# Convolution sums on ScalarE and GpSimd, column combinations on VectorE alone, projection products between the last attention steps

## The chip, the core and the metric

The kernel runs on one core of a Trainium2 chip. That core has five engines that work side by side, each through its own queue in order: TensorE (PE in the profile, its weight loads PEld), VectorE (DVE), ScalarE (ACT), GpSimd (POOL) and SyncE (SP, which here issues most of the transfers). The metric is the device time of one execution in microseconds. Before the change it is 2511.84 us, the median of three runs (2492.11 to 2514.36).

## What is computed

The input is `x`, eight images of 32 by 32 positions with 256 channels, all in float32. Cut to what matters:

```python
# layer 0: convolution beside attention with relative positions, on the group-normalized input
g = group_norm(x)
conv = conv3x3(g, conv_w) + conv_b                         # 192 channels
k, q, v = split(g @ qkv_w + qkv_b)                         # 8 heads of 8
w = softmax(q @ k.T + rel_w(q) + rel_h(q))                 # 1024 x 1024 per head and image
x = x + concat([conv, (w @ v) @ attn_w + attn_b])
# layer 1: attention of one head, then two experts per image
t = x.reshape(8, 1024, 256)
n = layer_norm(t)
t = t + n + softmax(Q(n) @ K(n).T / sqrt(128)) @ V(n) @ W_o + b_o
n = layer_norm(t)
out = t + layer_norm(n + top2_experts(n)) 
```

## The kernel before

The images go one after the other through two layers, and the experts of all images follow at the end. One image takes some 243 us. In program order it has these stages:

1. `conv_layer_attention(b)`, the convolution layer's attention. It works in four units of four heads and 512 queries. A loop over `s` (44 steps) runs three things at a distance of ten and eleven steps. `Unit.score` (L588, then the maximum by DVE at L596) finds the maxima of a unit. `Unit.weigh` (L628, exponentials by ACT at L636) makes the weights, and `Unit.gather` (L645) makes the products with the values. For the first ten steps there is nothing to weigh, and products of the convolution stand in between (`conv.run`). In the last eleven steps there is nothing to score, and there the steps of `norm_steps` (the group normalization of the next image) are done through `ahead`. After the last step `settle` divides the last unit by its sums: it transposes `os` to `pa` (L670), DVE takes reciprocals `rc` (L673) and writes `at` (L674). Then `at` is transposed (`tpa`, L744), copied to `aT` (L745), and multiplied by the output projection (`pp`, L750). DVE adds that to the image `T[b]` (L751).
2. `attention_layer(b)`, the second layer's attention. It begins with a normalization over channels: statistics (L762, L86 to L90), then eight tiles `n` (L773) that PE transposes to `tpn` (L777) and ACT copies to `nT` (L781). POOL adds each `n` to `T[b]` (L778). Then come projections (L793, L809), scores (L830), exponentials, transposes (L850) and products (L861, L873). At the end POOL makes a sum over tokens (L913, L915).

While image b is in stage 2, work of image b+1 is put between its steps. `combine()` makes the combinations `gdif` of columns for the convolution (`by_fours`: the convolution along x is done by a scheme with six products for four columns). `fill(us)` takes steps of the generator `input_steps` until the given number of microseconds is used up. These are in turn four products `pk` (L394, for keys and queries, which go to `kq` at L403 by ACT and L410 by DVE, and by 16 transfers on SP to the patterns `km`), eight steps of `pvv` (L425, values, which DVE adds to `vall` at L433), eight pieces of `prel` (L464, position terms, copied by DVE at L476 and ACT at L478, after each of which four or five products of the convolution are run) and four steps of `tpw` (L489, transposes, copied to `rwq` by ACT and DVE in turn). The amounts that a step returns (`yield 0.86, False`) are its assumed duration and whether it is a piece after which convolution products follow.

The convolution itself (`conv_steps`) has two halves `r` of three pairs. A pair is two groups of six products (L511) into one PSUM tile `pc`. After each pair the six-products scheme is undone: the two groups become sum and difference, and these are added with weights to the four column groups `four` of `T[b]`. The first half of an image's convolution runs in the normalization of the image before, with `pc` in the pool `po_tile`, which has one buffer. The second half runs in the first ten steps of its own attention, with `pc` in `st_tile`, which has three. Image 0 does both halves there.

The order of PE's instructions is the order of the program text (`manual_schedule` for PE). On DVE, ACT, POOL and SP a planner orders the instructions when the program is built, by estimated durations and by the order of the text. Before the loop over the images DVE's order is by hand as well; there image 0's combinations are made, with all of `by_fours` on DVE. PSUM tiles come from pools: `st_tile` three buffers, `lg_tile` two, `po_tile` one.

## Time and profile before

| | us |
|---|---|
| median of three runs | 2511.84 |
| lowest and highest run | 2492.11, 2514.36 |
| the profiled execution | 2486.52 |
| its span, first to last instruction | 2483.7 |
| DVE busy | 1531.3 (62%) |
| ACT busy | 995.2 (40%) |
| POOL busy | 501.5 (20%) |

The page comes from one execution. Its groups give, for one line of the program and one engine, the count, the busy time and the mean duration. After the bar stands how long the engine was idle before these instructions and what ended most of that. The groups that the change touches:

```profile
L511 PE MATMUL pc<-convw,gdif 128*128 128x192 f32 x1152 | 235.8, 347 | 18.9 <-DVE sd L535 8.6
L350 DVE SCALAR_TENSOR_TENSOR gdif<-x 128x128 f32<-128x128 f32 x64 | 46.5, 796 | 0.0
L527 POOL TENSOR_TENSOR T<-T,sd 128x384 f32<-128x384 f32 x32 | 31.3, 1003 | 63.7 <-DVE sd L525 63.6
L745 DVE COPY aT<-tpa 64x512 f32<-64x512 f32 x16 | 10.8, 678 | 1.9 <-PE tpa L744 1.1
```

The first line says: 1152 products of the convolution, 235.8 us together, and PE idle for 18.9 us before them, of which 8.6 ended when DVE had written `sd`. A timeline gives instructions in order of time with merged repeats; `[0.93 <-ACT os L662]` means that the engine was idle for 0.93 us and what it then had was `os`, written by ACT. PEclk is the granted clock of TensorE, 1.00 for full rate.

### The profile page before, as it was taken

To read this page: it belongs to the slowest core of one execution; us is meant where nothing else is said; L and a number is where in the kernel's file an instruction comes from. 1 tells how busy PE (TensorE), PEld (TensorE's weight loads), DVE (VectorE), ACT (ScalarE), POOL (GpSimd) and SP (SyncE) were. 2 spreads that over 40 slices of the span, in tenths; PEclk is the share of its full clock that TensorE was granted. 3 is DMA by queue.
4 is the path that set the end of the run, shared out by engine and by line. 5 is a ranking of instruction groups with operands and counts; after the bars stand their busy time and mean duration, and the time that the engine had idled before them with its cause. 6 is when DMAs were issued, how large, how long until landed. Compare 5 with 4: busy or idle time off the path is not lost. (4 is left out here: it accounts for less than half of the span.)

```text
span 2483.7 us, 41827 instructions
## 1 busy us (share of the span) xinstructions
PE 2338.0 (94%) x17273; PEld 1313.9 (53%) x17273; DVE 1531.3 (62%) x2681; ACT 995.2 (40%) x1661; POOL 501.5 (20%) x434
## 2 busy tenths in 40 slices
PE   5999999999989999999999999999998869999998
PEld 4535643564356436643663366336632646666665
DVE  7776487648754875587568746774684444444443
ACT  2254336433643364346334632462256323332232
POOL 3103120402040204111320132022200132222221
PEclk7999999999999999999999999999999979999999
DMA  4520242134213412241224032403240032221110
GB/s 123 80 39 25 40 97 38 36 48 81 33 37 51 85 26 48 57 81 13 53 57 81 9 57 68 71 3 57 51 71 3 1 124 77 76 68 68 68 60 26
DMA packets 71469, 135.83 MB, mean 55 GB/s; under 512 B 12000, under 2 KB 24168, under 8 KB 69232
## 3 DMA queue, kind: packets, MB, share of 16 engines
q1 hardware_dynamic: 65488, 115.47, 23.4%
q0 software_dynamic: 3056, 15.73, 1.8%
q8 instruction: 136, 2.23, 0.4%
q10 hardware_dynamic: 2736, 1.97, 0.3%
q14 instruction: 53, 0.43, 0.1%
HBM read 53.43 MB, written 25.17 MB: 32 GB/s over the span
## 5 line engine op out<-in xcount | busy, mean ns | idle before, releaser
L596 DVE TENSOR_REDUCE my<-lg 128x32 f32<-128x1024 f32 x512 | 618.5, 1223 | 153.6 <-PE st L628 126.0
L636 ACT ACTIVATE PT<-st 128x512 f32<-128x512 f32 (+1 forms) x944 | 541.6, 632 | 412.3 <-PE st L628 407.9
L628 PE MATMUL st<-F,km 32*128 32x512 f32 x2048 | 547.5, 644 | 17.0 <-DMA F<-mb 11.7
L588 PE MATMUL lg<-km,F 24*128 24x512 f32 x2048 | 536.5, 642 | 11.4 <-DVE my L596 7.0
L645 PE MATMUL po<-PT,vall 128*32 128x256 f32 (+1 forms) x3200 | 316.7, 455 | 2.4 <-ACT PT L636 2.4
L588 PEld LDWEIGHTS lg<-km,F 24*128 24x128 f32 x2048 | 155.6, 184 | 191.3 <-issue 109.7
L511 PE MATMUL pc<-convw,gdif 128*128 128x192 f32 x1152 | 235.8, 347 | 18.9 <-DVE sd L535 8.6
L511 PEld LDWEIGHTS pc<-convw,gdif 128*128 128x128 f32 x1152 | 190.3, 195 | 90.4 <-issue 62.9
L645 PEld LDWEIGHTS po<-PT,vall 128*32 128x32 f32 x3200 | 67.0, 108 | 315.0 <-issue 280.9
L628 PEld LDWEIGHTS st<-F,km 32*128 32x128 f32 x2048 | 178.7, 184 | 97.6 <-issue 45.2
L1214 PE MATMUL phd<-n2T,w 128*128 128x512 f32 x512 | 223.8, 595 | 0.0
L1231 PE MATMUL py<-w,hT 128*128 128x256 f32 x1024 | 223.6, 379 | 0.0
L1231 PEld LDWEIGHTS py<-w,hT 128*128 128x128 f32 x1024 | 194.6, 190 | 33.3 <-issue 7.7
L311 POOL TENSOR_TENSOR T<-T,l0b 128x2048 f32<-128x2048 f32 x8 | 36.3, 4539 | 712.9 <-PE tpx L304 712.9
L1238 DVE TENSOR_TENSOR r<-py,n 128x256 f32<-128x256 f32 x64 | 27.1, 423 | 213.0 <-PE py L1231 213.0
L1214 PEld LDWEIGHTS phd<-n2T,w 128*128 128x128 f32 x512 | 97.0, 191 | 115.0 <-issue 107.8
L861 PE MATMUL po<-pt,qkv 128*128 128x256 f32 x512 | 116.6, 381 | 11.3 <-DVE pt L853 11.3
L839 DVE TENSOR_REDUCE nm<-lg 128x1 f32<-128x1024 f32 x64 | 78.1, 1221 | 77.8 <-PE lg L830 77.8
L1221 ACT ACTIVATE hT<-phd,b1c 128x512 f32<-128x512 f32 x128 | 86.3, 686 | 96.5 <-PE phd L1214 96.3
L830 PE MATMUL lg<-qkv 128*128 128x512 f32 x256 | 119.1, 593 | 0.0
L861 PEld LDWEIGHTS po<-pt,qkv 128*128 128x128 f32 x512 | 96.6, 190 | 36.2 <-DVE pt L853 13.2
L778 POOL TENSOR_TENSOR T<-T,n 128x256 f32<-128x256 f32 x64 | 47.2, 743 | 270.5 <-DVE n L773 270.5
(256 smaller groups left out, 2615.7 us busy)
## 6 DMA issues: line engine op xcount, KB each, us to landing
F<-rh SPq DMA_DIRECT2D x256, 128.0 KB
F<-kq SPq DMA_DIRECT2D x256, 64.0 KB
F<-rwd SPq DMA_DIRECT2D x256, 64.0 KB
w<-in_L_ffn_W_dram SPq DMA_DIRECT2D x32, 512.0 KB
rwd<-rw SPq DMA_DIRECT2D x16, 512.0 KB
Td<-T POOLq DMA_DIRECT2D x8, 1024.0 KB, 8.3
T<-Td SPq DMA_DIRECT2D x8, 1024.0 KB
out_dram<-yo SPq DMA_DIRECT2D x16, 512.0 KB
```

The source lines that it names most:

```text
L511: nc.tensor.matmul(pc[:, v, :], lhsT=gflat[:, 2 * pair + v, kc, at : at + P], rhs=convw[:, 2 * pair + v, dy, kc * CO : (kc + 1) * CO], sta ...
L588: nc.tensor.matmul(lg[:, a, :], lhsT=self.F[r : r + 24, a, 0, i * P : (i + 1) * P], rhs=KM[self.g][r : r + 24, a].rearrange("p e k -> p (e ...
L596: nc.vector.tensor_reduce(my[:, :, hl], lg.rearrange("p a (y x) -> p y a x", y=WW), AX.XY, ALU.max)
L628: nc.tensor.matmul(st[:, i, :] if len(heads) > 1 else st, lhsT=KM[self.g][r : r + 32, a, e, :], rhs=self.F[r : r + 32, a, e, :], start=Tru ...
L636: nc.scalar.activation(self.pts[j][:, hs, :], st, AF.Exp)
L645: nc.tensor.matmul(self.po[32 * hl : 32 * hl + 32, cols], lhsT=vall[:, j, h * (DH + 1) : h * (DH + 1) + 32], rhs=self.pts[j][:, hl, cols], ...
L830: nc.tensor.matmul(lg[:, h, :], lhsT=qk[0][:, i * P : (i + 1) * P], rhs=qk[1][:, h * 512 : (h + 1) * 512], start=True, stop=True,)
L839: nc.vector.tensor_reduce(nm, lg, AX.X, ALU.max, negate=True)
L861: nc.tensor.matmul(po[:, 0:IB], lhsT=v1[:, jc, :], rhs=pt[:, jc, :], start=jc == 0, stop=jc == NT - 1)
L1214: nc.tensor.matmul(phd, lhsT=ws[k][0][:, kc, f * P : (f + 1) * P], rhs=n2T[:, kc, q * 512 : (q + 1) * 512], start=kc == 0, stop=kc == KC - 1,)
L1221: nc.scalar.activation(hT[:, k * NF + f, :], phd, AF.Gelu, bias=b1c[:, f, k * B + b : k * B + b + 1])
L1231: nc.tensor.matmul(py, lhsT=hT[:, k * NF + f, j * P : (j + 1) * P], rhs=ws[k][1][:, f, :], start=k == 0 and f == 0, stop=k == TOPK - 1 and ...
```

## The change

Three parts. First, `by_fours` has no other engine to choose: its sums and differences of two tensors, which were on POOL for images 1 to 7, are on DVE for all.

Second, the sums after a pair of convolution products. Before, ACT copied one group and DVE made sum and difference out of PSUM and part of the additions to `four`, POOL the others. Now ACT copies both groups to `m`, and POOL makes all sums from there, with scalings of the second pair by ACT.

Third, `input_steps` of the next image is made before the attention of this one, and a function `more(n)` takes n of its steps. Two `pk` steps stand ahead of the last `settle` and two behind it, and four steps of `pvv` stand ahead of `pp`. One of the two copies `aT` goes to ACT. The first `fill` in the second layer has 4.5 in place of 7.5.

```diff
-        def by_fours(xn, other):
+        def by_fours(xn):
-            two = other.tensor_tensor
+            two = nc.vector.tensor_tensor
...
                             if v and i == n - 1:
-                                if pair < 2:
-                                    neg = work.tile([P, CO], FP, tag="neg", name="neg")
-                                    sd = work.tile([P, 2, CO], FP, tag="sd", name="sd", bufs=2)
-                                if pair == 0:
-                                    nc.scalar.copy(neg, pc[:, 1, :])
-                                    nc.vector.tensor_tensor(sd[:, 0], pc[:, 0, :], neg, ALU.add)
-                                    nc.vector.tensor_tensor(sd[:, 1], pc[:, 0, :], neg, ALU.subtract)
-                                    for h in range(2):
-                                        nc.gpsimd.tensor_tensor(
-                                            four[:, 2 * h : 2 * h + 2], four[:, 2 * h : 2 * h + 2], sd, ALU.add
-                                        )
-                                elif pair == 1:
-                                    nc.scalar.mul(neg, pc[:, 1, :], 2.0)
-                                    nc.vector.scalar_tensor_tensor(
-                                        sd[:, 0], neg, 0.5, pc[:, 0, :], ALU.mult, ALU.add
-                                    )
-                                    nc.vector.scalar_tensor_tensor(
-                                        sd[:, 1], pc[:, 0, :], 2.0, neg, ALU.mult, ALU.subtract
-                                    )
-                                    nc.gpsimd.tensor_tensor(four[:, 0:2], four[:, 0:2], sd, ALU.add)
-                                    nc.vector.scalar_tensor_tensor(
-                                        four[:, 2:4], sd, 4.0, four[:, 2:4], ALU.mult, ALU.add
-                                    )
+                                m = work.tile([P, 2, CO], FP, tag="m", name="m", bufs=2)
+                                nc.scalar.copy(m, pc)
+                                add = nc.gpsimd.tensor_tensor
+                                if pair == 2:
+                                    add(four[:, 0:4:3], four[:, 0:4:3], m, ALU.add)
                                 else:
-                                    nc.vector.tensor_tensor(four[:, 0:4:3], pc, four[:, 0:4:3], ALU.add)
+                                    sd = work.tile([P, 2, CO], FP, tag="sd", name="sd")
+                                    add(sd[:, 0], m[:, 0], m[:, 1], ALU.add)
+                                    add(sd[:, 1], m[:, 0], m[:, 1], ALU.subtract)
+                                    if pair:
+                                        nc.scalar.mul(sd[:, 1], sd[:, 1], 2.0)
+                                    add(four[:, 0:2], four[:, 0:2], sd, ALU.add)
+                                    if pair:
+                                        nc.scalar.mul(m, sd, 4.0)
+                                        sd = m
+                                    add(four[:, 2:4], four[:, 2:4], sd, ALU.add)
...
+                if g == NU:
+                    more(KC)
                 if 0 <= g and g <= NU and l == 0 and g > 0:
                     units[g - 1].settle(at)
+                if g == NU:
+                    more(KC)
...
-                nc.vector.tensor_copy(
-                    aT[:, q * 512 : (q + 1) * 512], tp[0:DK].rearrange("p j t -> p (j t)")
-                )
+                dst, src = aT[:, q * 512 : (q + 1) * 512], tp[0:DK].rearrange("p j t -> p (j t)")
+                if q == 0:
+                    nc.vector.tensor_copy(dst, src)
+                else:
+                    nc.scalar.copy(dst, src)
+            more(NT // 2)
...
-            fill(7.5)
+            fill(4.5)
...
+                steps = iter(()) if last else input_steps(b + 1, held)
+
+                def more(n):
+                    for _ in range(n):
+                        next(steps, None)
+
                 conv_layer_attention(
...
-                steps = iter(()) if last else input_steps(b + 1, held)
```

More of the change, by code (lines that the diff above doesn't have):

```diff
@@ L684, with conv_layer_attention @@
         LAG = 2
-        def conv_layer_attention(b, units, kq, rh, rwd, rwq, conv, early, ahead):
+        def conv_layer_attention(b, units, kq, rh, rwd, rwq, conv, early, ahead, more):
             at = work.tile([P, NT, DK], FP, tag="at", name="at")
@@ L962 @@
             reld_steps()
-            other = chain(by_fours(held["xn"], nc.vector), conv_weights(taps))
+            other = chain(by_fours(held["xn"]), conv_weights(taps))
             for _ in steps:
@@ L992 @@
                     iter(()) if last else ahead(),
+                    more,
                 )
                 conv = Conv(b + 1)
-                steps = iter(()) if last else input_steps(b + 1, held)
                 def fill(us):
@@ L1009, in combine @@
                     if not last:
-                        for _ in by_fours(held["xn"], nc.gpsimd):
+                        for _ in by_fours(held["xn"]):
                             pass
```

## The prediction

> **What bounds the kernel now.** The page comes first: its rows of busy time say TensorE (PE) carries the span, and the row PEclk says where it runs at half rate.

> ```profile
> PE 2338.0 (94%) x17273; PEld 1313.9 (53%) x17273; DVE 1531.3 (62%) x2681; ACT 995.2 (40%) x1661; POOL 501.5 (20%) x434
> PEclk7999999999999999999999999999999979999999
> ```

> So a change pays only where PE stands idle, runs at half clock, or is paced by another engine. From one layer end (L751 starts) to the next an image takes some 243 us, with 10 to 12 us of PE gaps. Three places belong to this change. The first is the end of the convolution layer's attention; here is the timeline of all engines at the end of image 2 (start, us, engine, line, idle before):

> ```profile
> 702.55 0.66 PE L670 MATMUL pa<-ident,os 128*128 128x128 f32 x4 [0.93 <-ACT os L662]
> 702.58 2.16 DVE L350 SCALAR_TENSOR_TENSOR gdif<-x,gdif 128x128 f32<-128x128 f32 x4
> ...
> 703.05 0.60 PE L744 MATMUL tpa<-ident,at 128*64 128x128 f32 x4
> ...
> 704.87 0.24 DVE L673 RECIPROCAL rc<-pa 128x16 f32<-128x16 f32 x1
> ...
> 705.49 1.06 PE L744 MATMUL tpa<-ident,at 128*64 128x128 f32 x4 [1.84 <-DVE at L674]
> ...
> 706.48 3.67 PE L750 MATMUL pp<-aw,aT 64*128 64x64 f32 x16
> ```

> PE waits 0.93 for ACT's `os`, then 1.84 because DVE ends the column combinations (L350) before it takes up `rc`. Afterwards the same four transposes take 1.06, not 0.60, and `pp` 3.67, not 2.00 as in image 1: half clock. The table of busy time by stretch, seven image ends, tells the same (last fields: PEclk, DMA share, GB/s):

> ```profile
> 457.00:475.00 18.00, 16.44 (x159) 11.22 (x155) 13.37 (x44) 7.18 (x11) 5.89 (x7) 1.00 0.04 6
> 700.00:718.00 18.00, 14.93 (x61) 9.47 (x61) 12.29 (x41) 4.91 (x8) 4.41 (x5) 0.72 0.02 3
> ```

> Images 0, 2, 4, 6 end at a clock of 0.81, 0.72, 0.81, 0.72, the odd ones at 1.00; there the wait before L744 is about 0.3 only. The second place is the normalization that follows, where a pair of convolution products waits for its one PSUM buffer (timeline of PE):

> ```profile
> 481.78 0.56 PE L511 MATMUL pc<-convw,gdif 128*128 128x192 f32 x2 [1.16 <-DVE sd L525]
> ...
> 491.71 1.21 PE L511 MATMUL pc<-convw,gdif 128*128 128x192 f32 x6 [1.23 <-DVE sd L535]
> ```

> The third is the first eight score steps, before any exponentials. DVE is busy 23.81 of the 26 us from 556 to 582, and the waits of PE's weight loads from 555 to 591 name it:

> ```profile
> PEld lg L588 <- DVE my L596: 5.8, 9, 1.1
> ```

> DVE paces PE there, so DVE work taken out of this stretch is time.

> [...] in image 0, where DVE alone makes the combinations, four `gdif<-x` take 1.25 us; at 449.31 with Pool beside it eight take 6.27. [...] The trace shows the half rate after gaps of 0.9 and 1.8 us in a row, so low use is enough; cause and phase are not shown. [...] The trace has no GpSimd instruction on PSUM.

> **The change part by part.** Seven image boundaries (0 to 6) have a next image; all sums are over these.

> *Combinations on DVE.* Pool loses 12 sums per image, 13 us. DVE gains them: in image 0 they read 0.63, 0.63, 0.45, 0.46, 0.66, 0.68, 0.51, 0.51, 0.61, 0.56, 0.60, 0.55, together 6.85. The 24 fused ones fall from 12.5 (449.31 to 461.62, with Pool) to 7.0 (image 0's rows). In wall time, image 0's run from 34.77 to 49.48, less the three copies between, is 12.3 us, against 12.5 (449.31 to 461.82). `xn`'s last L333 loses its 1.54 for 0.74. So DVE comes free some 0.9 us earlier, at about 460.9: no cost and no gain by itself, as long as `rc` is needed later than that.

> *Products between the last steps.* Moved up: eight PE instructions of `pk` (3.5 us, 464.95 to 468.49), the two ACT and two DVE writes of `kq` (0.77 and 0.73 each), 16 transfers `km<-kq` on SP (image 0: 11.03 us for 16, with nothing behind them until `rwd<-rw`), and half of `pvv` (1.84 of 3.68). Nothing on POOL's queue moves. `xn` is ready at 449.4, 10 us before. The first `pk` half (1.75) covers the 0.93 for `os`. The second covers `pa` to `at` (0.24 + 0.29 and hand-offs; `pa` now ends near 463.4, after DVE's 460.9). `pvv` covers the copies of `aT`, one of which goes to ACT (0.59). Gain: 7 x 0.93, plus the waits before L744 (1.87, 0.33, 1.84, 0.31, 1.86, 0.26, 1.87, sum 8.3), **15 us**. The moved `kq` writes stand ahead of `aT` on DVE and ACT, 0.7 us each, under the same cover.

> *What their old cover hid.* `fill(7.5)` becomes `fill(4.5)`: behind `pp`, PE has half of `pvv` (1.84) and two pieces of `prel` with their convolution steps (2.6 and 2.9), 7.3 us. DVE needs 0.69 + 2.71 + 0.63 + 0.15, ACT about 0.3, DVE 0.18, then `vall` 0.69 and `n` 0.41: 5.8, or 6.8 if a copy of `prel` (1.06) slips in. Cost 0. But one `prel` piece fewer is left for the eight later slots, so two `tpw` steps now fall between the last transposes, when both `tpn` tiles hold two of three PSUM buffers. The second waits for the first's copy (0.59 ACT), the third partly (0.69 DVE): 0.6 to 1.3 per image, I take 0.9, **-6 us**. Bounds 0 (the free buffer comes earlier) and -12.

> *Convolution sums, normalization half.* One ACT copy frees the PSUM pair. A 128x384 copy is not in the trace; between 128x192 (0.32) and 128x512 (0.59) I read 0.48. The gap of 1.16 and 1.23 (0.32 + 0.36 + 0.35 and hand-offs) becomes about 0.6: 7 x 1.15, **8 us**.

> *Convolution sums, score half.* DVE loses 0.36 + 0.35 (L524, L525) and 0.35 + 0.35 + 0.56 (L532, L535, L539), 1.97 us, inside the DVE-paced stretch; L543 (0.55) lies behind a transfer `F<-mb` and pays nothing. Pool works here longer, and L600 beside it took 0.62, not 0.29: -0.5. 7 x 1.45, **10 us**; bounds 5 and 14. Image 0's half is paced by PE: 0.

> *What is added.* Pool per half: four 192-wide sums (between 0.40 for 128 and 0.73 for 256, I take 0.57) and five 384-wide (1.00), 7.3 against 3.3 now. ACT: three copies, and scalings of 192 and 384, 2.3 against 0.65. ACT has 9.7 busy of 36 us in the normalization, and 2.2 of 36 in the score stretch. New waits: the scaling waits for Pool's two sums, 1.2 us or more if Pool holds an `L778` (0.74) or the running sum of the token mean; behind it on ACT are copies of `prel` and `rwq`. The next use of such a buffer is a piece of 2.6 us or more away: 0. On Pool the sums stand ahead of `T += n` (L778), which frees DVE's two `n`; a hold-up of 3.1 us is under two slots of 3.2. Scoring itself has no exponentials on ACT until 591.3.

> *Clock.* The four half-rate segments at even ends make up (1 - 0.81) x 18 x 2 and (1 - 0.72) x 18 x 2, 34 half-rate us in all, so at most 17 us. Other low spots remain (448, 578), and their phase moves. I take **10**; bounds -10 and 17.

> Sum: 15 - 6 + 8 + 10 + 10 = 37 us. Against the profiled execution's own 2486.5 that is 2449.5. The median of the runs, 2511.84, stands 25 us above it; the same amount gives **2475**.

> **Rivals.** *Given back* (chance 0.28): gaps close but PE waits shortly afterwards, at the `tpw` steps, for ACT behind a Pool wait, or in another half-rate window. For it: low clock turns up at 448 in odd images instead of at their end, at 578 too. Against: PE is nearly solid between. With 15 + 8 + 5 gained, 12 lost at `tpw` and 5 in the clock: 11 us, 2500. That the moved products do not run early, since PE has a written order but DVE and ACT don't, belongs here: it leaves 8 + 10 - 6, also 2500.

> *DVE late behind the combinations* (0.12, slower): DVE's order is planned from estimated costs. With twelve more DVE instructions the planner may leave some of the 12.3 us behind `at`. They then stand ahead of statistics and `n`, whose cover is now 7.3, down from 9.7. It decides once more than 1.5 us of them spill. With 8 us spilled, PE waits 6.5, and a half-rate segment of 10.24 costs 5: 7 x 11.5 = 80, less 37, so 43 slower, 2555. Against: today they are wholly ahead of L673, with 12 us from `xn` to `rc`.

> **How the numbers follow.** The steps hold (0.60): 2445 to 2490 by their bounds, 2475 likeliest. A difference under 1% (2487 to 2537) is about what a measurement of this kernel cannot tell from none. Faster: most of the first case, a little of the second, 0.58. Same: the second and edges of both others, 0.31. Slower: 0.11. The range 2442 to 2510 leaves out the slow rival and the extremes.

> **What would show it.** Right: no gap before L670 and L744's second group, clock 1.00 at all image ends, gaps of 0.6 between L511 groups, no DVE rows of `sd`, `gdif` rows of 0.31 each. Wrong: a PE wait before `tpn` named by `n`; waits at `tpw` over 1.3; L511 or L464 held by an ACT instruction that itself waits for POOL; DVE busy as before between score steps.

## The result and the profile after

The changed kernel takes **2483.31 us** (median of 11 runs, 2480.10 to 2486.32) where the kernel before takes 2519.15 beside it (11 runs, 2490.25 to 2534.49): a ratio of **0.9895 [0.9861, 0.9928]**. The ratios here, and the table of two parts below, leave out runs more than 1.5% above the fastest of their kernel (three of the 11 here, nine of 45 of before and two of 20 of `e3_more` further down), which is why this ratio is nearer to one than the two medians are. The profiled execution of the changed kernel took 2484.71 us, its span 2482.9 at a mean granted clock of 0.966. That of before took 2486.52 at 0.970. So the two profiled executions are within 2 us of each other, while the medians are 36 apart. The whole study turns on that difference.

From the page of the changed kernel: the row of busy time, the row of the granted clock, and two groups of instructions (busy us, mean ns of one | idle before, releaser).

```profile
PE 2351.1 (95%) x17273; PEld 1333.3 (54%) x17273; DVE 1482.9 (60%) x2661; ACT 1028.4 (41%) x1717; POOL 476.4 (19%) x446
...
PEclk8998999899999999999899999999999979999999
...
L511 PE MATMUL pc<-convw,gdif 128*128 128x192 f32 x1152 | 245.9, 358 | 11.0 <-ACT m L520 8.7
...
L520 ACT COPY m<-pc 128x384 f32<-128x384 f32 x48 | 23.0, 478 | 254.3 <-PE pc L511 254.3
```

The same 17273 matmuls keep PE busy 13.1 us longer than before (2338.0), and the row of the clock now has an 8 in the slices in which images 0, 1 and 4 end. The new ACT copy takes 0.478 us, as estimated, and the wait before `pc` falls from 18.9 to 11.0.

The table of busy time by stretch shows the image ends again (after the window: length, busy us of PE, PEld, DVE, ACT, POOL with counts; then PEclk, DMA share, GB/s):

```profile
457.00:475.00 18.00, 17.37 (x144) 13.12 (x143) 10.02 (x34) 6.80 (x11) 0.00 (x0) 0.82 0.08 15
700.00:718.00 18.00, 17.36 (x148) 12.82 (x141) 12.15 (x41) 6.19 (x11) 0.00 (x0) 0.80 0.08 15
942.00:960.00 18.00, 17.37 (x147) 12.84 (x142) 12.11 (x41) 6.52 (x11) 0.00 (x0) 0.81 0.09 16
```

PE is busy 17.4 of 18 us, against 16.44 and 14.93 before, and yet the clock is low at **every** end: 0.74, 0.91, 0.90 and 0.88 in the same windows at images 0, 4, 5 and 6. Before, it was 1.00 at the odd ones. The timeline of PE at the end of image 1 (start, us, engine, line, count, idle before) shows both the gain and the loss:

```profile
459.07 1.98 PE L394 MATMUL pk<-x,qkvw 128*128 128x512 f32 x4
460.89 0.60 PE L661 MATMUL pa<-ident,os 128*128 128x128 f32 x4
461.32 1.88 PE L394 MATMUL pk<-x,qkvw 128*128 128x512 f32 x4
463.04 1.04 PE L739 MATMUL tpa<-ident,at 128*64 128x128 f32 x8
464.42 2.00 PE L425 MATMUL pvv<-qkvw,x 128*128 128x64 f32 x16 [0.34 <-DVE aT L742]
466.35 2.00 PE L748 MATMUL pp<-aw,aT 64*128 64x64 f32 x16
468.27 3.53 PE L425 MATMUL pvv<-qkvw,x 128*128 128x64 f32 x16
471.73 1.93 PE L464 MATMUL prel<-kq,bdw 32*64 32x32 f32 x64
473.59 2.93 PE L511 MATMUL pc<-convw,gdif 128*128 128x192 f32 x8
...
485.24 0.59 PE L511 MATMUL pc<-convw,gdif 128*128 128x192 f32 x2 [0.62 <-ACT m L520]
...
503.05 0.66 PE L489 MATMUL tpw<-ident,rw 128*128 128x128 f32 x4 [0.68 <-ACT rwq L493]
...
504.49 1.09 PE L489 MATMUL tpw<-ident,rw 128*128 128x128 f32 x8 [0.57 <-ACT nT L779]
```

The waits for `os` and `at` are gone. One of 0.34 is left. But the second half of `pvv` takes 3.53 us where the first takes 2.00, `prel` 1.93 where it takes 1.26 at full clock, eight `pc` 2.93 where they take 1.57: half rate (from 468.46 to 482.11 the granted clock is 0.50), with PE busy almost without a break.

DVE's timeline (same columns), the end of the combinations and three rows of the score stretch after image 2:

```profile
459.20 0.55 DVE L382 TENSOR_TENSOR gdif<-gdif,x 128x224 f32<-128x224 f32 x1
461.52 0.26 DVE L664 RECIPROCAL rc<-pa 128x16 f32<-128x16 f32 x1 [1.77 <-PE pa L661]
...
808.74 4.81 DVE L587 TENSOR_REDUCE my<-lg 128x32 f32<-128x1024 f32 x4 [0.27 <-PE lg L579]
813.59 0.71 DVE L591 TENSOR_TENSOR my<-my,rwq 128x128 f32<-128x128 f32 x1
...
821.00 4.81 DVE L587 TENSOR_REDUCE my<-lg 128x32 f32<-128x1024 f32 x4 [0.28 <-PE lg L579]
```

DVE is done with the combinations at 459.75, before `pa` exists, and waits 1.77 us for it. In the score stretch DVE now waits 0.27 and 0.28 us for PE, which it did not before.

**Two parts of a time.** Each run lists its span and its mean granted clock. I take the product of the two as what the span would be with no half rate in it, and span x (1 - clock) as what half rate cost. This is an estimate, good to a few us only: it counts half of all time at half rate as lost, also that in which PE is idle and that of the thinnest products, though `prel` takes 1.93 us at half rate and 1.26 at full rate, not 2.52. So a kernel with much half rate in thin products gets too low a first part and too high a second. These are medians over the runs of each kernel, in us; the runs of before are those that ran beside the experiments, and the kernels e1 to e10 are described below:

```
kernel            runs   clock (lowest-highest)   at full rate   cost of half rate
before             36    0.962 (0.951-0.972)        2410.9          96.5
after              11    0.963 (0.962-0.966)        2390.1          91.8
e1_sums             4    0.972 (0.972-0.974)        2403.7          69.2
e2_comb            12    0.962 (0.956-0.970)        2406.2          95.1
e3_more            18    0.954 (0.948-0.961)        2401.7         115.8
e7_no_more          4    0.977 (0.976-0.977)        2399.5          57.7
e4_late             4    0.971 (0.966-0.972)        2397.7          71.6
e5_dense            4    0.976 (0.972-0.978)        2406.2          59.2
e10_after_again     4    0.964 (0.962-0.966)        2391.6          90.6
e8_rows             4    0.975 (0.968-0.977)        2372.2          60.8
e6_mixed            4    0.979 (0.978-0.981)        2374.5          52.2
e9_mixed_again      4    0.979 (0.978-0.982)        2375.7          51.0
```

Read the first two rows: the change takes 20.8 us out of the work and waits, and 4.7 out of the half rate of a median run. The profiled execution of before, at 0.970, lost only (1 - 0.970) x 2483.7 = 74.5 to half rate; of the 56 runs of before on record only one, 2484.82, was faster. In the 36 runs of before, span and clock go together (correlation -0.98): their spread of over 40 us is a spread of the clock. The changed kernel has hardly any.

### The profile page after: what moved, and what is told of

Its sections match the earlier page's. It is cut to its first block, busy times and chain, and to the rows that moved or that the text cites. A ratio compares the mean times of both kernels' runs of the same rounds, so it can differ in the third digit from the quotient of the medians.

```text
span 2482.9 us, 41840 instructions
## 1 busy us (share of the span) xinstructions
PE 2351.1 (95%) x17273; PEld 1333.3 (54%) x17273; DVE 1482.9 (60%) x2661; ACT 1028.4 (41%) x1717; POOL 476.4 (19%) x446
## 3 DMA queue, kind: packets, MB, share of 16 engines
q10 hardware_dynamic: 2736, 1.97, 0.3%
## 5 line engine op out<-in xcount | busy, mean ns | idle before, releaser
L511 PE MATMUL pc<-convw,gdif 128*128 128x192 f32 x1152 | 245.9, 358 | 11.0 <-ACT m L520 8.7
L511 PEld LDWEIGHTS pc<-convw,gdif 128*128 128x128 f32 x1152 | 198.3, 202 | 81.8 <-issue 61.2
L520 ACT COPY m<-pc 128x384 f32<-128x384 f32 x48 | 23.0, 478 | 254.3 <-PE pc L511 254.3
```

Of the source, the lines that this page charges most:

```text
L511: nc.tensor.matmul(pc[:, v, :], lhsT=gflat[:, 2 * pair + v, kc, at : at + P], rhs=convw[:, 2 * pair + v, dy, kc * CO : (kc + 1) * CO], sta ...
```

## The experiments

**One part alone, three times.** Each kernel is the one before with one of the three parts.

`e1_sums`: the sums by ACT and Pool.

```diff
-                                if pair < 2:
-                                    neg = work.tile([P, CO], FP, tag="neg", name="neg")
...
+                                m = work.tile([P, 2, CO], FP, tag="m", name="m", bufs=2)
+                                nc.scalar.copy(m, pc)
+                                add = nc.gpsimd.tensor_tensor
...
```

> The kernel before with the new convolution sums alone (ACT copy, sums on POOL). If the sums carry what I gave them, the pc gaps in the normalization fall from 1.16 and 1.23 to 0.62 each and the score stretch to the first st shortens by about 0.7 us per image (what the changed kernel's profile shows, 32.24 to 31.55): 7 x 1.8 = 13 us, ratio about 0.995. The half clock at image ends stays where it is before, at even images or wherever the phase puts it. Rival: POOL's sums hold ACT or PE elsewhere, and the time is that of before or more.

`e2_comb`: the combinations by DVE alone.

```diff
-            two = other.tensor_tensor
+            two = nc.vector.tensor_tensor
```

> The kernel before with the column combinations on DVE alone. Expected: DVE free about 2 us earlier at the image end, so the wait before the second group of tpa (1.84 at even images) goes, and with it the half clock that follows it if idleness brings it: 7 x 1 us plus up to 17, ratio 0.990 to 0.998. If thin products bring the half clock, it stays at some image ends though the wait is gone.

`e3_more`: the moved products, with one `aT` copy on ACT and the shorter fill.

```diff
+                if g == NU:
+                    more(KC)
                 if 0 <= g and g <= NU and l == 0 and g > 0:
                     units[g - 1].settle(at)
+                if g == NU:
+                    more(KC)
...
+            more(NT // 2)
...
-            fill(7.5)
+            fill(4.5)
```

> The kernel before with the moved products alone (more, one aT copy on ACT, fill 4.5). Theory A, a run of thin products (tpa, pvv, pp, pvv, prel, 64 columns or fewer) in a row lowers the clock: half rate of 10 to 14 us at every image end as in the changed kernel, so little or no gain, ratio 0.995 to 1.003. Rival B, idle gaps lower the clock: with the gaps covered the half rate disappears or is rarer than before, ratio 0.985.

Measured against one set of runs of before (median 2514.37): `e1_sums` 2474.74, ratio **0.987 [0.9785, 0.9955]**; `e2_comb` 2504.08, **1.0001 [0.9966, 1.0037]**; `e3_more` 2520.38, **1.0029 [1.0, 1.0057]**. The sums alone are no worse than the whole change, and better than the 0.995 expected of them; the combinations alone miss the 0.990 to 0.998 expected. The moved products alone bring nothing, although the table says that they take 9.2 us out of the part at full rate: half rate takes 19.3 back. The timeline of PE of `e3_more`, end of image 1, has the same picture as the changed kernel:

```profile
469.31 2.00 PE L425 MATMUL pvv<-qkvw,x 128*128 128x64 f32 x16 [0.34 <-DVE aT L751]
471.24 2.00 PE L757 MATMUL pp<-aw,aT 64*128 64x64 f32 x16
473.17 2.94 PE L425 MATMUL pvv<-qkvw,x 128*128 128x64 f32 x16
476.04 1.93 PE L464 MATMUL prel<-kq,bdw 32*64 32x32 f32 x64
477.90 2.93 PE L511 MATMUL pc<-convw,gdif 128*128 128x192 f32 x8
```

Half rate sets in during the second `pvv` (2.94 us for it, 2.00 for the first), after some 5 us of `pvv` and `pp`, without a gap; from 469 to 487 PE is busy 17.07 of 18 us and the clock is 0.81.

**The other way round.** `e7_no_more` is the changed kernel without its third part.

```diff
-                if g == NU:
-                    more(KC)
...
-                if g == NU:
-                    more(KC)
...
-            more(NT // 2)
...
-            fill(4.5)
+            fill(7.5)
```

> The changed kernel without the moved products (no more, both aT copies on DVE, fill 7.5): sums and combinations only. If the moved products as placed cost time, this is faster than the changed kernel: 2465 to 2480, with half rate at image ends in fewer than half of the images, and no wait of 1.84 before the second group of tpa. If the parts only work together: 2490 or more.

2458.99 us (2455.49 to 2459.85), ratio 0.9813 [0.9732, 0.9894]: 24 us **faster** than with the moved products, and below the 2465 that was its lowest forecast. In its profile three of the seven image ends have half rate, as forecast. The experiments ran in three groups, e1 to e4, e5 to e7 and e8 to e10; the changed kernel (2483.31, and 2483.91 in the third) and `e6_mixed` (2428.29 and 2428.60) came out alike in two of them, so I compare across. From `e7_no_more` to the changed kernel the part at full rate falls by 9.4, as from before to `e3_more` (9.2), and the cost of half rate rises by 34.1.

**What makes the clock fall.** In the kernel before, `pp` is followed by eight records of 512-column products `pk`. In the changed one `pvv` (64 columns), `pp` (64 columns, 64 rows), `pvv` and `prel` (32 columns, 32 rows) stand in a row, 7 to 8 us. Two kernels put dense work back. `e4_late` moves up the first half of `pk` only; the other half and all of `pvv` are behind `pp` again.

```diff
-                if g == NU:
-                    more(KC)
...
-            more(NT // 2)
...
-            fill(4.5)
+            fill(7.94)
```

> The changed kernel with only the first pk half moved up; the second pk half (512 columns, dense) and all of pvv stay behind pp, with fill 7.94 for the same steps. Theory A: tpa and pp are short before dense pk follows, so the half rate at the image ends goes or becomes rare; the gaps before tpa (about 0.9) and pp (about 0.4) come back, 1.3 us per image; net 3 to 5 us per image faster than the changed kernel, some 2455. Rival B (idle gaps): half rate at every end again or more, 2490 or above.

2472.32 us (2468.74 to 2483.59), ratio 0.987 [0.9781, 0.996]. The part at full rate is 7.6 longer than in the changed kernel, since a wait for `at` is back (1.06 at the end of image 1), and the half rate costs 20.2 less. That is slower than the 2455 forecast, and the half rate is not gone: in the profile one window of 3.4 us is left at five of the seven image ends, and 17.1 us at image 5.

`e5_dense` leaves the changed kernel as it is and *adds* work: two products of 512 columns (two records each) in each image but the last, whose results are read by nobody.

```diff
+            def dense():
+                if b + 1 < B:
+                    rhs = convw[:, 0].rearrange("p d n -> p (d n)")[:, 0:512]
+                    nc.tensor.matmul(po_tile("dense"), lhsT=ident, rhs=rhs, start=True, stop=True)
+
...
+            dense()
...
+            dense()
```

> The changed kernel plus two useless dense products (512 columns, 128 rows, never read) per image, one between the moved half of pvv and pp, one behind pp: 2 x 0.86 us more PE work per image, 12 us in all. Theory A (thin products in a row, measured as columns times rows streamed per 3.4 us, lower the clock): the half rate of 10 to 14 us at each image end goes or shrinks to 3.4, so the stretch from the last gather to the first tpn falls from 21 to 22.5 us to about 18 to 19, and the kernel is faster for more work: 2455 to 2465. Rival B (idle gaps lower the clock) and rival C (phase alone): half rate as before, 12 us slower, 2495.

2468.53 us (2462.47 to 2475.2), ratio 0.9848 [0.9765, 0.993], against 2483.31 without the useless work (2455 to 2465 were forecast). The timeline of PE at the end of image 2, and the stretch around it in the table by stretch:

```profile
704.21 2.00 PE L425 MATMUL pvv<-qkvw,x 128*128 128x64 f32 x16 [0.34 <-DVE aT L747]
706.05 1.08 PE L738 MATMUL dense<-convw,ident 128*128 128x512 f32 x2
707.06 2.00 PE L754 MATMUL pp<-aw,aT 64*128 64x64 f32 x16
708.98 1.13 PE L738 MATMUL dense<-convw,ident 128*128 128x512 f32 x2
709.94 1.89 PE L425 MATMUL pvv<-qkvw,x 128*128 128x64 f32 x16
711.77 1.25 PE L464 MATMUL prel<-kq,bdw 32*64 32x32 f32 x64
```

```profile
698.00:716.00 18.00, 17.66 (x216) 12.76 (x214) 9.91 (x32) 5.62 (x9) 1.20 (x2) 1.00 0.10 18
```

The second `pvv` takes 1.89 and `prel` 1.25: full rate, clock 1.00. The wait of 0.34 and PE's busy time, 17.66, are those of the changed kernel (17.36 to 17.66 in such a stretch; from 702 to 720 it has the same 17.66, at a clock of 0.74), so idleness was not what set the clock. The dense products cost 16 us at full rate (12 by their own durations) and save 33 of half rate. One rival is left, where the image ends lie on the grid of 3.41 us on which the clock changes (see the count below): an image of `e5_dense` lasts 71.0 such windows, so all its gathers end at the same place in one, 0.27 to 0.30 behind an edge. The traces answer it. In the changed kernel the gathers of images 1 and 4 end at 0.27 and 0.28, the same place, and 13 us of half rate follow each. Not all half rate goes: outside the image ends, images 1 to 6 have 41.0 us of it in `e5_dense` and 10.2 in the changed kernel, as single windows some 11 us before the gathers' end and in the first score steps; why these come is not shown.

**The same with useful work.** `e6_mixed` separates the thin products by convolution steps of the next image, and the second half of `pk` stands ahead of `pp`, where half of `pvv` stood. For that their combinations must be ready, so `by_fours` runs right after `norm_steps`, earlier than before, and the next `Conv` is made before the attention. Pieces of `prel` bring three convolution steps each, not four or five, since twelve now stand further up.

```diff
                 if g == NU:
-                    more(KC)
+                    nxt(4)
...
-            more(NT // 2)
+            more(KC)
...
-            combine()
-            fill(4.5)
+            for us in (1.7, 1.7, 1.0):
+                dense(4 if us > 1.0 else 0)
+                fill(us)
...
                     yield from norm_steps(b + 1, held)
+                    for _ in by_fours(held["xn"]):
+                        pass
...
-                            conv.run(5 - len(pieces) % 2)
+                            conv.run(3)
```

> The changed kernel with the order of PE at the image end so that dense products stand between thin ones: pk half, settle, four convolution steps, tpa, pk half, pp, four convolution steps, half of pvv, four steps, half of pvv; three convolution steps behind each prel piece instead of four and five; combinations emitted behind the group normalization. Same work as the changed kernel. Theory A: no half rate at image ends, and the gaps stay covered: last gather to first tpn about 17.5 us, with 25.5 to pq, 2450 to 2460, faster than any so far. Rival B or C: half rate of about 10 us at most ends, 2480 or more.

**2428.29 us** (2427.1 to 2429.25), ratio **0.9695 [0.9615, 0.9775]**; it beats both kernels and its forecast of 2450 to 2460. The timeline of PE, end of image 2, and two rows of the groups by shape over the whole run:

```profile
689.92 2.00 PE L748 MATMUL pp<-aw,aT 64*128 64x64 f32 x16
691.85 1.57 PE L511 MATMUL pc<-convw,gdif 128*128 128x192 f32 x8
693.25 1.89 PE L425 MATMUL pvv<-qkvw,x 128*128 128x64 f32 x16
694.99 1.52 PE L511 MATMUL pc<-convw,gdif 128*128 128x192 f32 x8
696.34 1.89 PE L425 MATMUL pvv<-qkvw,x 128*128 128x64 f32 x16
698.16 1.25 PE L464 MATMUL prel<-kq,bdw 32*64 32x32 f32 x64
```

```profile
L511 PE MATMUL pc<-convw,gdif 128*128 128x192 f32 x1152 | 236.4, 347 | 3.1 <-ACT convw L280 2.2
...
L489 PE MATMUL tpw<-ident,rw 128*128 128x128 f32 x128 | 19.3, 300 | 3.3 <-ACT nT L780 3.3
```

No gap and full rate: from 689 to 707 PE is busy 18.00 of 18 us at a clock of 1.00. A pair of convolution groups is 24 products (1152 over 48 copies), or 12 steps; with 12 steps up front and 3 per piece every pair ends where a piece ends, so that `prel` (1.25 us) covers the ACT copy (0.478): the wait of `pc` for `m` (8.7 us in the changed kernel) is gone.

**Which of it does what.** `e6_mixed` changes several things, so `e8_rows` has the same instructions and moves only the convolution steps: eight ahead of `tpa`, none between `pp` and the two halves of `pvv`, four behind them. It ran beside a repeat of `e6_mixed` and of the changed kernel.

```diff
-                    nxt(4)
+                    nxt(8)
...
-            for us in (1.7, 1.7, 1.0):
-                dense(4 if us > 1.0 else 0)
-                fill(us)
+            fill(3.4)
+            dense(4)
+            fill(1.0)
```

> The same instructions as e6_mixed on every engine, the same early combinations and three convolution steps to each prel piece; only the place of 8 of the 12 convolution steps at the end of an image differs, so that pp and the two pvv halves (5.7 us of thin products) stand in a row. Theory 'thin runs lower the clock': 7 to 14 us of half rate between the gathers and the first transposition of n in most images, against 0.00 in e6_mixed, and some 3 to 5 us more per image: 2450 to 2470 us. Rival 'the early combinations and the shorter convolution pieces made the gain of e6_mixed': no half rate there or at no cost, and within 8 us of e6_mixed, 2422 to 2436 us.

> The kernel of e6_mixed a second time, beside e8_rows on one chip: 2424 to 2434 us on both theories, no half rate at the ends of the images.

> The changed kernel as it is, beside e8_rows and e9_mixed_again on one chip: 2475 to 2490 us, 10 to 14 us of half rate at the end of every image. If e8_rows comes out near this, the early combinations bring nothing; if it comes out near e9_mixed_again, they bring all.

On one chip: `e8_rows` 2435.62 (2433.8 to 2452.39), `e9_mixed_again` 2428.60 (2426.03 to 2429.47), `e10_after_again` 2483.91 (2481.14 to 2486.8). The row of thin products costs 7 us here, not the 20 or more that I had expected, which lies inside the rival's range. The timeline of PE of `e8_rows`, end of image 2, is one of only two of its seven image ends with half rate (a clock of 0.81 from 691 to 709, with PE busy 18.00 of 18 us):

```profile
691.11 2.00 PE L748 MATMUL pp<-aw,aT 64*128 64x64 f32 x16
693.03 5.31 PE L425 MATMUL pvv<-qkvw,x 128*128 128x64 f32 x32
698.14 2.87 PE L511 MATMUL pc<-convw,gdif 128*128 128x192 f32 x8
```

My own sums over images 1 to 6 of five profiles, us ("whole images" is from the `pq` of image 0 to that of image 6; "at half rate" is the time at a granted clock of 0.50, of which I count half as lost):

```
                       gathers' end to first tpn  first tpn to pq   whole images 1-6
kernel                 length  at half rate       length            length  at half rate  PE idle
before                 104.5       27.3           158.6             1460.9      51.2        64.8
after                  129.9       67.5           141.5             1459.6      78.5        50.4
e5_dense               110.5        0.0           141.2             1454.0      41.0        51.2
e8_rows                106.8       13.7           122.8             1419.8      27.3        37.4
e6_mixed               100.0        0.0           122.8             1413.0      13.7        37.3
```

From the changed kernel to `e8_rows`, 39.8 us: PE idle falls by 13.0, and 51.2 us at half rate less are worth about 25.6. So what the two orders share does most of it: `pk` and convolution steps in the thin row, which shorten it from some 8 to 5.7 us, the earlier combinations, and three steps to each piece. What each of these is worth by itself was not tried. The last step, no row at all, gives another 6.8, for 13.6 us of half rate less. In `e6_mixed` the gathers end at three places of the 3.41 us grid (about 0.2, 0.6 and 0.9 of a window behind an edge), and no end has half rate.

**A count over ten profiles.** The edges of the half-rate stretches lie on a grid of 3.41 us. In the clock records of the profiles of before and after the granted clock is 1.00 or 0.50, never between. Every stretch at 0.50 lasts a whole number of 3.413 us (3.41, 6.83, 10.24, 13.65, 17.07, 23.89 or 27.31), except the last one of each record (6.99 and 6.05), and all edges ahead of that one lie within 0.001 us of one grid. The table of busy time by stretch of the changed kernel, cut at this grid, behind the gathers of image 1:

```profile
461.64:465.05 3.41, 3.07 (x18) 1.89 (x16) 2.42 (x5) 1.57 (x3) 0.00 (x0) 1.00 0.06 12
465.05:468.46 3.41, 3.41 (x31) 3.28 (x29) 0.08 (x1) 0.00 (x0) 0.00 (x0) 1.00 0.14 24
468.46:471.87 3.41, 3.41 (x22) 3.29 (x23) 3.31 (x10) 0.00 (x0) 0.00 (x0) 0.50 0.14 24
471.87:475.29 3.42, 3.42 (x69) 3.36 (x70) 1.41 (x12) 1.70 (x3) 0.00 (x0) 0.50 0.10 19
475.29:478.70 3.41, 3.41 (x69) 2.91 (x69) 0.25 (x1) 0.00 (x0) 0.00 (x0) 0.50 0.31 46
478.70:482.11 3.41, 3.41 (x12) 3.11 (x11) 1.33 (x3) 1.05 (x1) 1.51 (x2) 0.50 0.00 0
482.11:485.53 3.42, 2.80 (x73) 2.32 (x73) 0.41 (x1) 0.48 (x1) 1.00 (x2) 1.00 0.02 5
```

PE is busy for all of the window from 465.05 to 468.46, with `pvv` and `pp`, and the four windows behind it have half rate. For each such window of the profiles of before, after and `e1_sums` to `e8_rows`, from 100 to 1900 us, I added up what its products stream: 0.43 us for 512 columns (the spacing of the `phd` products, 0.429), in proportion to the columns, and to the rows of 128 in use. Windows at full rate, by that share and by the rate of the window that followed:

```
share of the window   followed by half rate   followed by full rate
under 0.30                     18                       1
0.30 to 0.42                   80                      27
0.42 to 0.48                    4                     323
0.48 and over                   7                    4623
```

Twelve `pvv` and sixteen `pp` make 0.31, as at the ends of the changed kernel; thirty `pvv` alone would make 0.47, in the class where full rate follows 323 of 327 windows. This would explain why half rate comes with the 5.7 us row in `e8_rows` at only two of seven ends, where a window would hold enough of `pp`. The weights of the count are mine, its borders were chosen on these profiles, and the 27 and the 7 show that it is not the exact rule. Two things support it. A border on PE's busy time puts 94 of these windows wrong even at its best and one on columns alone 88, where 0.42 above puts 39 wrong. And in the two profiles that the count left out, of `e9_mixed_again` and `e10_after_again`, 16 of 18 windows under 0.42 are followed by half rate and 1 of 997 above; these are repeats of kernels in the count, though.

## Why the prediction was right, and where it was not

**The sum.** 2475 was forecast, 2483.31 came, and "faster" came by 1.05%, just over the 1% that the prediction drew as its line and with an interval that crosses it. But the sum was made against the profiled execution, which should have fallen by 37 to 2449.5 and fell by 1.8, with 25 us added back as a constant. Both steps were wrong, by 35 and by 27 us in opposite directions; that 2475 came within 8.3 us is luck. The 25 us were not a constant: some 22 of them (96.5 less 74.5) were half rate that the profiled execution of before happened to escape (a clock of 0.970 against a median of 0.962). The changed kernel has no such luck and no such spread; its median lies 1.4 below its profiled execution. Compared by the table, the parts at full rate were to give 15 - 6 + 8 + 10 = 27 and gave 20.8, and the clock was to give 10 and gave 4.7.

**Moved products, 15 less 6 at `tpw`.** Near, at full rate: 9 forecast, 9.2 (`e3_more`) and 9.4 (`e7_no_more` to the changed kernel) measured by the split. The gap before `pa` is gone, that before `tpa` as well, 0.34 remains before the first `pvv`. At `tpw` PE waits 0.68 and 0.57, within the 0.6 to 1.3 stated; over the run of `e3_more` it is 8.7 us against 0.9 before, 7.8 for the 6 forecast. In the same two profiles the waits before `pa` fall from 7.4 to 0.9 and those before `tpa` from 8.6 to 0.7, and 2.4 new ones stand before `pvv`: 12.0, for 15 forecast. Less 7.8 that is 4.2 and not 9.2. The other 5 are not found among the waits; that the split gives too low a part at full rate is one candidate.

**Clock, "I take 10; bounds -10 and 17".** This is the step that failed. It took the low clock at the even ends for a consequence of the gaps, which would go with them; its own sign of being right, a clock of 1.00 at all image ends, came at none. From one profiled execution to the other the half rate of images 1 to 6 rose from 51.2 to 78.5 us, some 13.7 us of time lost where 10 were to be won. By the medians the half rate still costs 4.7 less, but only as the difference of two effects that were not forecast: the sums and combinations lower its cost by 38.8 (before to `e7_no_more`), and the moved products raise it by 34.1, far outside the bounds. The prediction had the evidence in its own words, "half rate after gaps of 0.9 and 1.8 us in a row, so low use is enough" (from 701.44 to 704.85, a window of the 3.41 us grid, PE is busy 1.28 of 3.41 us, and the three windows behind it are at 0.50), but did not ask how low the use is in the order that the change makes. It looked at idle time, and the row of thin products has none. In the changed kernel PE is busy 17.4 of 18 us at the ends of images 1 to 3, at a clock of 0.80 to 0.82.

**Sums, normalization half, 8.** Right: gaps of 0.62 each, and `pc` waits 7.9 us less.

**Sums, score half, 10 with bounds 5 and 14.** Too high. After image 2 the stretch from the first `my` to the first `mcol` shrinks by 0.73 us, not 1.45, which would be 5.1 in seven images, at the lower bound: 24.55 (from 804.18 to 828.73 before) against 23.82 (from 802.77 to 826.59). DVE's timeline, before and then after:

```profile
804.18 1.23 DVE L596 TENSOR_REDUCE my<-lg 128x32 f32<-128x1024 f32 x1 [0.58 <-PE lg L588]
...
815.10 0.62 DVE L600 TENSOR_TENSOR my<-my,rwq 128x128 f32<-128x128 f32 x1
...
828.73 0.25 DVE L609 TENSOR_SCALAR mcol<-mx 128x16 f32<-128x16 f32 x2
```

```profile
802.77 1.23 DVE L587 TENSOR_REDUCE my<-lg 128x32 f32<-128x1024 f32 x1 [0.58 <-PE lg L579]
...
826.59 0.25 DVE L600 TENSOR_SCALAR mcol<-mx 128x16 f32<-128x16 f32 x2
```

The five instructions of 1.97 us are gone, but from start to start they held DVE for 1.53 only, since each begins before the one ahead of it has ended. And PE comes next: it lets DVE wait 0.27 and 0.28 (a wait of 0.51 for `pmt` was there before). The sum with `rwq` takes 0.71 at 813.59, beside Pool's sum `acc<-acc,part` (813.42 to 814.14), and 0.29 at 825.85, with Pool idle; but before it took 0.62 at 815.10 already, beside the same sum of Pool's (814.84 to 815.57). In all the sums take 7.2 us out at full rate (`e1_sums`), for 18 forecast; the wait at `tpw` takes some back, for the first of it appears with them alone (0.9 us over the run before, 2.8 in `e1_sums`). What was not forecast is that they lower the cost of half rate by 27 against the median run of before. One part of it shows in the profiles: between the transposes of `n` and `pq`, images 1 to 6 have 6.8 us of half rate in `e2_comb` and 42.4 in `e3_more`, with the old sums and their gaps of 1.2, though none in the one profile of before; with the new sums it is at most 0.8 in every kernel. The count over windows fits that. A window of 3.41 us laid at every place between these transposes and `pq` holds a share under 0.42 at 9 to 10% of the places in the profile of before (0.33 at the least) and at none with the new sums (0.425 at the least); from `pq` to the end of the next gathers it is 1.4 to 1.9% of the places before and at most 1.0% with the new sums. By this estimate it would hang, with the old sums, on where an image lies on the grid how often half rate comes. No run tested this by itself, and how much of the 27 us it explains is open.

**Combinations, 0.** Right: 12.3 us of wall time as forecast (447.48 to 459.75), ratio 1.0001 in `e2_comb`. The 4.7 us that it takes out at full rate are near the 0.9 us per image by which DVE was to come free earlier; that this is their cause is not shown.

**The rivals.** "DVE late behind the combinations" fell: DVE waits 1.77 us for `pa`. "Given back" named the true mechanism among its three, "another half-rate window", but sized it at 5 us. That the new Pool and ACT work would hold PE up did not come about: an ACT scaling waited up to 1.4 us for Pool, and no PE wait names it (the wait of `tpw` for ACT's `rwq`, 4.7 us, is the same in `e3_more` with the old sums).

## What to carry to other kernels

Before filling a gap on TensorE, add up how many columns and rows the products in the new order stream per window of 3.41 us, and not only whether the engine is busy. In the ten profiles here half rate follows 98 of the 126 windows under a share of 0.42 and 11 of the 4957 above it, and a row of thin products cost more than the gaps that it filled: 34.1 us of half rate for 9.4 at full rate (`e7_no_more` to the changed kernel). Try to spread thin products among dense ones (2428.60 us in `e9_mixed_again`, 2435.62 with them in a row in `e8_rows`), and let groups that share one PSUM buffer end where other work follows (the 8.7 us for which `pc` waited for `m` are gone in `e6_mixed`). Before building a sum on one profiled execution, ask where in the spread of the runs it stands, and put the spread into two parts by span times clock.
